# One iteration re-ordered in a convolution, attention and expert kernel: scores and weighted values pulled apart, the second residual moved to the next iteration, the first deviations sent through DRAM

## The chip, the cores and the metric

The kernel runs on one core of a Trainium2 chip (trn2). The core has a matrix engine (TensorE, PE in the profile, with its weight loads as PEld), a vector engine (VectorE, DVE), a scalar engine (ScalarE, ACT), GpSimd (POOL) and a sync engine (SyncE, SP) that here only starts DMAs; POOL starts some too. Each engine takes its own instructions strictly in their order and waits on semaphores for the others. [...] The metric is the time of one execution on the device in microseconds, the median over several runs.

## The reference, cut to what matters

The input x has the shape 32 x 56 x 56 x 128. Layer 0 is a group norm, a batch norm reduced to its sign, and a 3 x 3 convolution with binary inputs and binary weights, with a residual. Layer 1 takes the 3136 tokens of each image, does a window attention (64 tokens, 4 heads of 32, causal) with a residual, and then an expert layer in which each of 64 experts picks the 8 tokens of an image with the largest softmax over tokens.

```python
x = x + _L0_conv_ref(_gn(x), L0_conv_gamma, L0_conv_beta, L0_conv_W)
t = _to_tokens(x)
t = t + _L1_attn_ref(_ln_t(t), L1_attn_w_qkv, L1_attn_w_proj, L1_attn_b_proj)
t = t + _L1_ffn_ref(_ln_t(t), L1_ffn_gate_w, L1_ffn_gate_b, L1_ffn_weight1, L1_ffn_weight2)
...
def _ln_t(v, eps=1e-5):
    m = jnp.mean(v, axis=-1, keepdims=True)
    s = jnp.var(v, axis=-1, keepdims=True)
    return (v - m) / jnp.sqrt(s + eps)
```

The two layer norms matter here. The kernel has the mean folded into centred weights, so that of each norm only the reciprocal deviation of a token is left to be multiplied in.

## The kernel before

**Stages.** A first stage reads all of x once for the statistics of the norms (line 292 on). The main loop (line 933) then does convolution, attention, the second residual and the gate's logits. A last stage, from line 1029, does the experts and adds their outputs to the rows they were picked from. All of this document is about the main loop and its two ends.

**Blocks.** The images are taken in 16 pairs, and each pair in 7 blocks (NB) of 8 image rows, which is 448 tokens of each of two images. That gives 112 blocks. A block is held as 7 units (NU) of 128 columns, 64 tokens of the one image and 64 of the other. In most tiles channels are on the partitions, so a deviation, which belongs to a token, must be spread over 128 partitions before it can be multiplied in.

**The pipeline of blocks.** Iteration n works on several blocks at once: it loads block n+6, makes the binary inputs of n+5 (`bits`), convolves n+3 (`conv`, `residual`), takes the statistics of n+2 (`norm1`), multiplies the deviations into n+1 and makes its queries, keys and values (`normalise`, `queries_or_keys`, `values`), does the attention of block n (`scores`, `attend`, `turn_out`, `project`, `norm2`) and the gate's logits of n-1 (`gate_logits`). The order in which the methods are called is the order of the instructions on PE, DVE, ACT, POOL and SP, since in the fast form of the loop (line 373) nothing reorders them.

**What one block passes through.** `bits` transposes a loaded block on PE (xT_ps, line 440), ACT makes xT and the thresholded input bn, DVE turns that into bits (lines 496 and 497). `conv` does nine products into one PSUM bank (cv), four at one place of the iteration and five at another. `residual` takes the sums out of PSUM (ACT, s2; DVE, s1) and adds them to xT, which gives yT (line 526). `norm1` transposes yT on PE (yt), DVE takes the statistics (line 433 and four small ones), POOL raises the variance to the power -0.5 (line 426). `normalise` spreads the deviations by seven transposes of a broadcast column on PE (rr, line 537) and multiplies (n1T, line 541). `scores` adds a mask by four products and then the 56 products of queries and keys (sc); ACT takes exp (pT). `attend` multiplies with the values (av), DVE divides (rs, ao). `turn_out` transposes ao (aoT_ps, with a copy by ACT), `project` multiplies with the projection's weights (pj) and adds the second residual on DVE (tT, line 679). `norm2` transposes tT (tt), ACT copies it (tok), DVE and POOL take its deviations, and tok is stored twice by DMAs, to the output on POOL's queue and to a scratch copy (toks) on SP's. `gate_logits` multiplies tT with the gate's weights (lg, copied by ACT).

**Steps of a finished pair.** When a pair's last block is done, its logits are worked on beside the next pair's blocks, in steps numbered j = 1 to 13, one per iteration (`step`, line 898): j = 1 ends the spreading of the second deviations over DRAM (`spread`, drow), 2 scales 3136 logits per partition, 3 finds the 8 largest, 4 their positions, 5 gathers the rows by eight indirect DMAs on POOL, 6 takes their statistics and the exps, 7 weighs them, 8 to 13 build the matrix that spreads expert outputs to rows (`shares`). Steps 8 to 13 of a pair fall into the same iterations as steps 1 to 6 of the next.

**PSUM.** Two single banks are held by cv and by lg; lg's bank also serves two small transposes (dT_ps in `spread`, pl in `turn_pooled`). All other tiles of a block rotate through three places of two banks each (`bank2`), so a new tile waits until the third tile before it has been read. An iteration of before takes 12 such tiles, in the order sc, sc, rr, av, xT_ps, qT_ps, aoT_ps, kT_ps, v_ps, pj, yt, tt.

**Zeros.** The matrix share, in DRAM, must be zero before the shares are stored. In iterations 1 to 8 SP starts one DMA of 1 MB each for it (line 942).

Of the kernel before, what the change touches and what calls it, by code (L numbers as in the profile page):

```python
# [30 lines left out]
def kernel(  # L31
# [40 lines left out]

    ident = const.tile([P, P], F32, name="ident")
# [9 lines left out]
    head1 = const.tile([P, HEADS, HD], F32, name="head1")  # L83
# [12 lines left out]
    g4 = const.tile([P, P // 4, 4], F32, name="g4")  # L96
# [12 lines left out]
    tri = const.tile([P, 2, P], F32, name="tri")  # L109
# [54 lines left out]
    with tc.tile_pool(name="prep", bufs=1) as prep, tc.tile_pool(  # L164
# [123 lines left out]


        TP = 2 * S // P  # L290
        x2 = x.rearrange("b h w c -> (b h w) c").rearrange("(n p j) c -> n p j c", p=P, j=TP)
        for pr in range(NPAIR):
            xb = xs.tile([P, TP, C], F32, name="xb")
            nc.sync.dma_start(out=xb, in_=x2[pr])
            st = xs.tile([P, 2, NB, 6], F32, name="st")
            for g in range(NB):
                pt = xps.tile([P, 2, 512], F32, name="pt").rearrange("p a (s c) -> p (a s) c", c=P)
                for j in range(NU):
                    nc.tensor.transpose(pt[:, j, :], xb[:, g * NU + j, :], ident)
                for i in range(2):  # L300
                    nc.vector.bn_stats(st[:, i, g, :], pt[:, :NU, i * WIN : (i + 1) * WIN])  # L301
            for i in range(2):
                nc.vector.bn_aggr(
                    mv[:, 2 * pr + i, :], st[:, i].rearrange("p g s -> p (g s)")
                )
            if pr == NPAIR - 4:
                group_norm(0, B - 8)
            if pr == NPAIR - 2:
                scaled(0, B - 8)
        group_norm(B - 8, B)  # L310
# [20 lines left out]


# [3 lines left out]

    share = dram.tile([NQ, P, NPAIR, 2, ES], F32, name="share")
    toks = [dram.tile([2, S, P], F32, name=f"toks{i}") for i in range(NPAIR)]
    eout = dram.tile([E, B, P], F32, name="eout")
    obias_d = dram.tile([P, NG, P], F32, name="obias_d")  # L340
    devs = [dram.tile([2, NB * NU, WIN], F32, name=f"devs{i}") for i in range(NPAIR)]
# [25 lines left out]
    def main_loop(fast):  # L367
        with ExitStack() as main:
# [41 lines left out]
            zero = first.tile([P, 4 * P], F32, name="zero")  # L410
            nc.gpsimd.memset(zero, 0.0)
# [46 lines left out]
            class Block:  # L458
# [16 lines left out]
                def bits(self):  # L475

                    pr, r = self.pr, self.r
                    xT_ps = turn(self.xb, "xT_ps")
                    self.xT = xTp.tile([P, 2, BT], F32, name="xT")
                    nc.scalar.activation(  # L480
                        self.xT.rearrange("c i (p j) -> c i p j", j=NU),
                        units(xT_ps).rearrange("c j (i p) -> c i p j", p=WIN),
                        AF.Identity, bias=conv_nb,
                    )
                    bn = w1.tile([P, 2, RB, W], F32, name="bn")
                    for i in range(2):
                        b = 2 * pr + i
                        nc.scalar.activation(  # L488
                            bn[:, i].rearrange("c h (g j) -> c h g j", j=NU),
                            units(xT_ps)[:, :, i * WIN : (i + 1) * WIN].rearrange(  # L490
                                "c j (h g) -> c h g j", h=RB
                            ),
                            AF.Identity, bias=thr_b[:, b : b + 1], scale=thr_a[:, b : b + 1],
                        )
                    bit = w1.tile([P, RB, W], FP16, name="bit")
                    nc.vector.tensor_scalar(bit, bn[:, 0], 0.0, 1.0 / FINE, ALU.is_ge, ALU.mult)
                    nc.vector.scalar_tensor_tensor(
                        hbits[pr % 2][:, 1 + r * RB : 1 + (r + 1) * RB, 1 : 1 + W],
                        bn[:, 1], 0.0, bit, ALU.is_ge, ALU.subtract,
                    )  # L500
# [15 lines left out]
                def residual(self):  # L516

                    cv = self.cv[:, :BT]
                    self.yT = yTp.tile([P, NU, P], F32, name="yT")

                    s2 = w1.tile([P, BT], I32, name="s2")
                    nc.scalar.activation(s2, cv, AF.Identity, bias=conv_mid)  # L522
                    s1 = w1.tile([P, BT], F32, name="s1")
                    nc.vector.tensor_sub(s1, s2, cv)  # L524
                    for i, t in enumerate((s1, s2)):
                        nc.vector.scalar_tensor_tensor(  # L526
                            of_image(self.yT, i), windows(t), conv_s2[:, i : i + 1],
                            windows(self.xT[:, i, :]), ALU.mult, ALU.add,
                        )

                def norm1(self):
                    self.rstd1 = unit_stats(units(turn(self.yT, "yt")), "ln1")

                def normalise(self):
                    rr = bank2("rr")
                    for u in range(NU):
                        nc.tensor.transpose(  # L537
                            units(rr)[:, u, :], self.rstd1[:, u : u + 1].to_broadcast([P, P]), ident
                        )
                    self.n1T = w1.tile([P, NU, P], F32, name="n1T")  # L540
                    nc.vector.tensor_mul(self.n1T, units(rr), self.yT)
# [125 lines left out]
                def project(self):  # L667

                    pj = bank2("pj")
                    for g in range(2):  # L670
                        for i in range(2):
# [4 lines left out]
                            )  # L676
                    self.tT = w1.tile([P, NU, P], F32, name="tT")
                    for i in range(2):
                        nc.vector.scalar_tensor_tensor(  # L679
                            of_image(self.tT, i), windows(pj[:, i, :BT]), bproj_c,  # L680
                            of_image(self.yT, i), ALU.add, ALU.add,
                        )
# [24 lines left out]
            class Pair:  # L707
# [9 lines left out]
                def spread(self, r0, r1):  # L717
# [4 lines left out]
                    dT = wp.tile([m, P], F32, name=f"dT{m}")  # L722
# [7 lines left out]
                    for i in range(2):  # L730
                        nc.sync.dma_start(
                            out=self.drow[i * E : (i + 1) * E, r0 * BT : r1 * BT],
                            in_=devs[self.pr][i : i + 1, r0 * NU : r1 * NU]
                            .rearrange("o m t -> o (m t)").to_broadcast([E, (r1 - r0) * BT]),
                        )
# [131 lines left out]
                def shares(self, ks):  # L867

                    if ks[0] == 0:
                        self.sh = gatep.tile([P, E, K], F32, name="sh")  # L870
# [27 lines left out]
                def step(self, j):  # L898
# [13 lines left out]
                    elif j == 8:  # L912
                        self.pool()
                        if self.pr < NPAIR - 2:
                            self.shares(range(0, 2))
                    elif j == 9:
                        self.shares(range(2, 3))
                    elif j == 10:
                        self.shares(range(3, 4))
                    elif j == 12:  # L920
                        self.shares(range(4, 6))
                    elif j == 13:
                        self.shares(range(6, 8))
# [9 lines left out]
            for n in range(-6, N + 1):  # L933
                this, nxt, conv, prev = at(n), at(n + 1), at(n + 3), at(n - 1)
# [4 lines left out]
                if at(n + 6):  # L939
                    at(n + 6).load()  # L940
                if 0 < n <= NQ:
                    nc.sync.dma_start(
                        out=share[n - 1].rearrange("p n i s -> p (n i s)").rearrange(
                            "p (a s) -> p a s", s=4 * P
                        ),
                        in_=zero.unsqueeze(1).to_broadcast([P, NPAIR * 2 * ES // (4 * P), 4 * P]),
                    )
# [20 lines left out]
                if n == N - 4:  # L968
                    parts = [Part(0, early)]
                    parts[0].load1()  # L970
                    parts[0].load2()
                if this:
# [3 lines left out]
                if nxt:  # L976
                    nxt.normalise()
                if prev:
                    prev.gate_logits(pairs[prev.pr])
                if 5 in ends:  # L980
                    ends[5].gather()
                if 7 in ends:
                    ends[7].put_rows()
                if this:
                    this.attend()
                if at(n + 5):
                    at(n + 5).bits()
# [6 lines left out]
                if 1 in ends and n < N:  # L994
                    ends[1].spread(NB - 1, NB)
                if nxt:
                    nxt.queries_or_keys(0)
                if this:
                    this.turn_out()
                if nxt:  # L1000
                    nxt.queries_or_keys(1)
                    nxt.values()
                if 8 in ends:
                    ends[8].turn_pooled(pcv.tile([P, 512], F32, name="pl", tag="lg")[:, :P])
                if 6 in ends:
                    ends[6].exps()
                for j, pair in steps:
                    pair.step(j)
                if n == N - 1:
                    pairs[this.pr].scale(0, NB - 2)  # L1010
                    pairs[this.pr].largest(0, NB - 2)
                if this:
                    this.project()
                if at(n + 2):
                    at(n + 2).norm1()
                if conv:
                    conv.conv(4, NTAP)
                    conv.residual()
                if this:
                    if this.r == 0:  # L1020
                        pairs[this.pr] = Pair(this.pr)
                    this.norm2(pairs[this.pr])
# [212 lines left out]
```

## Time and profile before

| | |
|---|---|
| median of 5 runs | 2471.09 us (2462.24 to 2475.05) |
| the profiled execution | 2466.99 us, of which the span is 2465.3 us |
| PE busy | 2177.6 us, 88% of the span |
| DVE busy | 1781.1 us, 72% |
| ACT busy | 1158.0 us, 47% |
| POOL busy | 814.4 us, 33% |
| granted clock of PE, mean | 0.95 |
| first stage | up to about 165 us |
| main loop, from the first weighted values (av) of block 0 to the last | 203 to 2168 us |

The page of the profile divides the span into 40 slices of 61.6 us; in the main loop PE is at 9 tenths or more in each of them. In the timeline a row is a run of equal instructions: its start, its length, the engine, the line, and in brackets the engine's idle time before it and who ended it. Matmuls overlap at their ends, so what a group costs PE is the distance from its start to the start of the next row.

### The profile page before, as it was taken

What the parts mean: (1) busy time and instruction counts of PE and PEld (TensorE: products, weight loads), DVE (VectorE), ACT (ScalarE), POOL (GpSimd) and SP (SyncE); (2) the same over time, 40 slices, a digit from 0 to 9 for tenths busy, and PEclk for the clock granted to TensorE, in tenths of its full rate; (3) what the DMA queues carried; (4) which work ended last, traced back from release to release, by engine and by line L of the source; (5) the groups of instructions that cost most, each with busy time, mean ns of one, the idle gap of its engine ahead of it and who ended that gap; (6) DMA issues with size and microseconds to landing.
All of it is one profiled execution on the core that took longest, in us unless ns stands there. A gap on an engine that the chain in (4) does not pass through costs nothing.

```text
span 2465.3 us, 82834 instructions
## 1 busy us (share of the span) xinstructions
PE 2177.6 (88%) x35865; PEld 1529.7 (62%) x35865; DVE 1781.1 (72%) x4974; ACT 1158.0 (47%) x1683; POOL 814.4 (33%) x772
## 2 busy tenths in 40 slices
PE   6769999999999999999999999999999999936342
PEld 5656666667676766676766666666666666613232
DVE  8965667777788878787877787878787878773221
ACT  0015555555555555555555555555555555422110
POOL 1011224232333333333332323233323232333555
PEclk9989999999999999999999999999999999967766
DMA  9933454645354545454544444545444444648762
GB/s 375 386 130 93 136 154 99 129 95 117 92 115 100 114 97 115 97 117 98 116 99 111 101 106 103 114 103 115 101 109 101 111 104 97 209 122 292 252 217 81
DMA packets 238300, 334.31 MB, mean 136 GB/s; under 512 B 50598, under 2 KB 175206, under 8 KB 231654
## 3 DMA queue, kind: packets, MB, share of 16 engines
q1 hardware_dynamic: 208102, 255.48, 37.1%
q0 software_dynamic: 27648, 72.38, 12.5%
q8 instruction: 285, 4.67, 0.8%
q10 hardware_dynamic: 2176, 1.05, 0.1%
q14 instruction: 89, 0.73, 0.1%
HBM read 195.14 MB, written 134.74 MB: 134 GB/s over the span
## 4 chain that ended last, share of the span: by engine, by line
PE 74%; DVE 7%; issue 6%; ACT 6%; POOL 5%; DMA 1%; POOLq 0%; SPq 0%; DVEq 0%; another core or an unknown queue 0%
PE cv L509 8%; PE av L639 8%; PE kT_ps L550 8%; PE pj L673 8%; PE v_ps L566 7%; PE sc L590 6%; POOL out_dram L1129 4%; PE xT_ps L440 4%; PE lg L701 4%; PE yt L440 4%; PE rr L537 4%; PE tt L440 4%; ACT bn L488 3%; DVE st L301 3%; PE qT_ps L550 3%
## 5 line engine op out<-in xcount | busy, mean ns | idle before, releaser
L426 POOL TENSOR_TENSOR ln_rstd<-ln_var,nhalf 128x7 f32<-128x7 f32 x112 | 167.6, 1496 | 960.1 <-DVE ln_var L423 615.4
L480 ACT ACTIVATE xT<-xT_ps,conv_nb 128x896 f32<-128x896 f32 x112 | 112.8, 1007 | 407.2 <-PE xT_ps L440 251.3
L426 POOL TENSOR_TENSOR devs<-ln_var,nhalf 128x7 f32<-128x7 f32 x112 | 165.7, 1479 | 268.9 <-DVE ln_var L423 268.9
L605 ACT ACTIVATE pT<-sc 128x896 f32<-128x896 f32 x224 | 193.3, 915 | 120.2 <-PE sc L590 120.2
L639 PEld LDWEIGHTS av<-vblk,pT 64*64 64x64 f32 x12544 | 195.5, 135 | 86.0 <-ACT pT L605 73.0
L509 PE MATMUL cv<-hbits,wconv 128*128 128x448 f16 x1008 | 236.8, 362 | 12.7 <-DVE s L524 6.3
L566 PEld LDWEIGHTS v_ps<-wqkvT,n1T 128*128 128x128 f32 x1568 | 192.7, 192 | 41.6 <-issue 41.6
L639 PE MATMUL av<-vblk,pT 64*64 64x33 f32 x12544 | 209.4, 221 | 6.0 <-issue 5.1
L522 ACT ACTIVATE s<-cv,conv_mid 128x448 int32<-128x448 f32 x112 | 70.8, 632 | 297.5 <-PE cv L509 219.6
L679 DVE SCALAR_TENSOR_TENSOR tT<-pj,bproj_c,yT 128x448 f32<-128x448 f32 x224 | 142.7, 679 | 92.5 <-PE pj L673 78.6
L550 PE MATMUL kT_ps<-n1T,wqkvT 128*128 128x448 f32 x448 | 197.7, 564 | 5.8 <-issue 1.3
L673 PE MATMUL pj<-aoT,wprojT 64*128 64x448 f32 x896 | 198.7, 562 | 1.1 <-ACT aoT L665 1.1
L566 PE MATMUL v_ps<-wqkvT,n1T 128*128 128x128 f32 x1568 | 193.1, 275 | 0.0
L550 PE MATMUL qT_ps<-n1T,wqkvT 128*128 128x448 f32 x448 | 188.3, 543 | 0.0
L433 DVE BATCH_NORM_STATS2 ln_st<-yt 128x6 f32<-128x128 f32 x784 | 165.5, 283 | 29.0 <-PE tt L440 14.6
L590 PE MATMUL sc<-qT,kT 32*64 32x64 f32 x12544 | 170.3, 238 | 0.5 <-issue 0.5
L692 POOL DMA_DIRECT2D out_dram<-tok x224 | 169.1, 756 | 0.1
L590 PEld LDWEIGHTS sc<-qT,kT 32*64 32x64 f32 x12544 | 154.4, 133 | 23.7 <-issue 23.7
L433 DVE BATCH_NORM_STATS2 ln_st<-tok 128x6 f32<-128x128 f32 x784 | 161.9, 278 | 4.9 <-ACT tok L687 4.9
L1129 POOL DMA_INDIRECT out_dram<-f_rows,rowidx x128 | 123.8, 967 | 103.3 <-DVE f_rows L1125 66.7
L488 ACT ACTIVATE bn<-xT_ps,thr_b,thr_a 128x448 f32<-128x448 f32 x224 | 149.3, 720 | 2.7 <-DVE thr_b L330 2.6
L526 DVE SCALAR_TENSOR_TENSOR yT<-s,conv_s,xT 128x448 f32<-128x448 f32 x224 | 143.5, 682 | 4.0
(187 smaller groups left out, 4094.4 us busy)
## 6 DMA issues: line engine op xcount, KB each, us to landing
xb<-in_x_dram SPq DMA_DIRECT2D x16, 3136.0 KB
xb<-in_x_dram SPq DMA_DIRECT2D x224, 224.0 KB
toks<-tok SPq DMA_DIRECT2D x224, 224.0 KB
out_dram<-tok POOLq DMA_DIRECT2D x224, 224.0 KB
u<-in_L_ffn_weight_dram SPq DMA_DIRECT2D x16, 2048.0 KB
drow<-devs SPq DMA_DIRECT2D x30, 672.0 KB
share<-zero SPq DMA_DIRECT2D x8, 1024.0 KB
grows<-rows SPq DMA_DIRECT2D x32, 256.0 KB
```

What stands on the lines that cost most here:

```text
L426: nc.gpsimd.tensor_tensor(rstd, var, nhalf[:, :n], ALU.pow)
L433: nc.vector.bn_stats(st[:, u, :], src[:, u, :])
L440: nc.tensor.transpose(units(t)[:, u, :], src[:, u, :], ident)
L488: nc.scalar.activation(bn[:, i].rearrange("c h (g j) -> c h g j", j=NU), units(xT_ps)[:, :, i * WIN : (i + 1) * WIN].rearrange("c j (h g) ...
L509: nc.tensor.matmul(self.cv[:, :BT], lhsT=wconv[:, t, :], rhs=hb[:, r * RB + kh : r * RB + kh + RB, kw : kw + W], start=(t == 0), stop=(t = ...
L550: nc.tensor.matmul(pp[:, a, :BT], lhsT=wqkvT[:, s, :], rhs=flat[:, a * BT : (a + 1) * BT], start=True, stop=True,)
L566: nc.tensor.matmul(units(vp)[:, u, :], lhsT=self.n1T[:, u, :], rhs=wqkvT[:, 2, :], start=True, stop=True,)
L590: nc.tensor.matmul(tiles[h // 2][part, h % 2, u * WIN : (u + 1) * WIN], lhsT=left[hp, u, part], rhs=right[hp, u, part], start=False, stop= ...
L605: nc.scalar.activation(pT, rows2(sc), AF.Exp, scale=HD ** -0.5)
L639: nc.tensor.matmul(av[h % 2 * WIN : (h % 2 + 1) * WIN, i, m * VW : (m + 1) * VW], lhsT=self.pT[h // 2][rows, h % 2, u, :], rhs=self.vb[row ...
L673: nc.tensor.matmul(pj[:, i, :BT], lhsT=wprojT[rows, g, :], rhs=self.aoT[rows, :, g, :], start=(g == 0), stop=(g == 1),)
L1129: put = nc.gpsimd.indirect_dma_start(out=of, out_offset=bass.IndirectOffsetOnAxis(ap=rowidx[:, n, q : q + 1], axis=0), in_=rows[q][:, n, : ...
```

## The change

The order of the calls within an iteration is new, and with it the distance of the blocks: the load is at n+7, bits at n+6, the convolution at n+4; the residual, the statistics of the first norm and their deviations are at n+3.

- **Scores and weighted values.** Between the scores of block n and its weighted values (av) now stand half of the convolution, the transposes of tT of block n-1 (tt) and of a loaded block (xT_ps), and the queries and keys of block n+1. The values of block n+1 come after.
- **Second residual.** `project` only makes the product pj. The residual itself is a new method `finish`, called at the start of the next iteration, followed there by `norm2` and `gate_logits` of that block.
- **Convolution's residual.** It is cut in two: `sums` reads PSUM in the convolution's own iteration, `residual` adds in the next.
- **First deviations.** `norm1` now takes the columns of yT with a step of seven tokens, so that the 128 x 7 deviations lie in token order, and POOL's queue stores them to DRAM (rdev). One iteration later `spread1`, on the same queue, loads them to all 128 partitions (rr, now in SBUF, 3584 bytes per partition). `normalise` multiplies yT by it. The seven transposes of line 537 are gone, and an iteration has 11 tiles in the rotation.
- **Steps of a pair.** Steps 1 to 7 (scale, largest, positions, statistics, weigh) stand between queries and keys and the weighted values, and so ahead of DVE's rs and ao; steps 8 to 13 (`step2`) stand ahead of s1. The shares are divided differently over them. The exps stand ahead of the exps of the scores on ACT.
- **The rest.** The zeros of share are written by eight DMAs at the end of the first stage. The loads of `drow` are cut into pieces of at most two blocks. Several tiles have moved between pools.

```diff
+        for q in range(NQ):
+            nc.sync.dma_start(out=share[q].rearrange("p n i s -> p (n i s)"), in_=zero)
         group_norm(B - 8, B)
...
                 def norm1(self):
-                    self.rstd1 = unit_stats(units(turn(self.yT, "yt")), "ln1")
+
+                    yt = bank2("yt")
+                    flat = self.yT.rearrange("c u p -> c (u p)").rearrange("c (p u) -> c u p", u=NU)
+                    for u in range(NU):
+                        nc.tensor.transpose(units(yt)[:, u, :], flat[:, u, :], ident)
+                    nc.gpsimd.dma_start(out=rdev[self.n], in_=unit_stats(units(yt), "ln1"))
+
+                def spread1(self):
+
+                    self.rr = w2.tile([P, NU, P], F32, name="rr")
+                    nc.gpsimd.dma_start(
+                        out=self.rr.rearrange("c u p -> c (u p)"),
+                        in_=rdev[self.n].rearrange("(o p) u -> o (p u)", o=1).to_broadcast([P, P * NU]),
+                    )
 
                 def normalise(self):
-                    rr = bank2("rr")
-                    for u in range(NU):
-                        nc.tensor.transpose(
-                            units(rr)[:, u, :], self.rstd1[:, u : u + 1].to_broadcast([P, P]), ident
-                        )
                     self.n1T = w1.tile([P, NU, P], F32, name="n1T")
-                    nc.vector.tensor_mul(self.n1T, units(rr), self.yT)
+                    nc.vector.tensor_mul(self.n1T, self.yT, self.rr)
...
+                def finish(self):
+
                     self.tT = w1.tile([P, NU, P], F32, name="tT")
...
+                if prev:
+                    if prev.r == 0:
+                        pairs[prev.pr] = Pair(prev.pr)
+                    prev.finish()
                 if this:
                     this.scores()
                 if conv:
                     conv.conv(0, 4)
                 if nxt:
                     nxt.normalise()
+                if at(n + 3):
+                    at(n + 3).residual()
                 if prev:
-                    prev.gate_logits(pairs[prev.pr])
+                    prev.norm2(pairs[prev.pr])
+                if at(n + 2):
+                    at(n + 2).spread1()
                 if 5 in ends:
                     ends[5].gather()
...
+                if at(n + 6):
+                    at(n + 6).bits()
+                for s in range(2):
+                    if nxt:
+                        nxt.queries_or_keys(s)
+                for j, pair in steps:
+                    pair.step(j)
                 if this:
                     this.attend()
-                if at(n + 5):
-                    at(n + 5).bits()
+                if prev:
+                    prev.gate_logits(pairs[prev.pr])
                 if this and this.r == NB - 1 and n < N - 1:
                     pairs[this.pr].spread(0, NB - 1)
...
                 if 1 in ends and n < N:
                     ends[1].spread(NB - 1, NB)
+                if at(n + 3):
+                    at(n + 3).norm1()
+                if 8 in ends:
+                    ends[8].turn_pooled(pcv.tile([P, 512], F32, name="pl", tag="lg")[:, :P])
                 if nxt:
-                    nxt.queries_or_keys(0)
+                    nxt.values()
                 if this:
                     this.turn_out()
...
+                if conv:
+                    conv.conv(4, NTAP)
+                    conv.sums()
+                if 6 in ends:
+                    ends[6].exps()
                 if this:
                     this.project()
```

## The prediction

> **What bounds the kernel now.** I read the shares of the page, then the main loop as one stretch, then PE's timeline of one iteration, and after that the rows of what the change moves. The line of the main loop has its length, then busy times of PE, weight loads, DVE, ACT and POOL, PE's granted clock, the share of the DMA engines and GB/s.
>
> ```profile
> PE 2177.6 (88%) x35865; PEld 1529.7 (62%) x35865; DVE 1781.1 (72%) x4974; ACT 1158.0 (47%) x1683; POOL 814.4 (33%) x772
> ```
> ```profile
> 203.00:2062.00 1859.00, 1818.77 (x32173) 1265.61 (x32172) 1445.66 (x4174) 1033.64 (x1330) 613.38 (x569) 0.99 0.47 110
> ```
> ```profile
> 482.42 0.59 PE L579 MATMUL sc<-masks,selw 64*128 64x448 bf16 x4
> ...
> 485.11 0.93 PE L537 MATMUL rr<-ident,ln_rstd 128*128 128x128 f32 x7
> 485.96 0.97 PE L701 MATMUL lg<-tT,gateT 128*64 128x448 f32 x4
> 486.87 1.84 PE L639 MATMUL av<-vblk,pT 64*64 64x33 f32 x112
> 488.63 0.98 PE L440 MATMUL xT_ps<-ident,xb 128*128 128x128 f32 x7
> 489.45 1.67 PE L550 MATMUL qT_ps<-n1T,wqkvT 128*128 128x448 f32 x4
> 490.96 0.93 PE L662 MATMUL aoT_ps<-ident,ao 128*128 128x128 f32 x7
> 491.94 1.77 PE L550 MATMUL kT_ps<-n1T,wqkvT 128*128 128x448 f32 x4
> 493.55 1.72 PE L566 MATMUL v_ps<-wqkvT,n1T 128*128 128x128 f32 x14
> 495.21 1.77 PE L673 MATMUL pj<-aoT,wprojT 64*128 64x448 f32 x8
> 496.91 0.98 PE L440 MATMUL yt<-ident,yT 128*128 128x128 f32 x7
> 497.73 1.12 PE L509 MATMUL cv<-hbits,wconv 128*128 128x448 f16 x5
> 498.69 0.93 PE L440 MATMUL tt<-ident,tT 128*128 128x128 f32 x7
> ```
>
> The reader is to see that PE has no gap: each group starts where the last ends, and attention starts at 486.87, 504.01 and 521.12, 17.13 us apart. 105 iterations from 203.0 take 1859 us, 17.71 each. The missing 0.57 per iteration, 4.0 per pair of images, is nearly all in one iteration of seven, j = 5, with the gather on POOL: it lasts 18.8 to 22.5 us. There PE, DVE and ACT wait while the gather is issued, and what delays them the trace does not say:
>
> ```profile
> 405.72 0.36 PE L579 MATMUL sc<-masks,selw 64*128 64x448 bf16 x2
> 407.80 0.36 PE L579 MATMUL sc<-masks,selw 64*128 64x448 bf16 x2 [1.72 <-DVE ln_st L433]
> ```
>
> So PE is the bound, and DVE, with 1446 of 1859 us (13.8 per iteration), is the next.
>
> **The change part by part.** I lay the new order out with the start-to-start times of that timeline, t = 0 at the masks: masks 0, scores 0.52, cv 1.91, tt 2.69, xT_ps 3.55, queries 4.37, keys 5.88, av 7.49, lg 9.25, yt 10.16, values 10.98, aoT_ps 12.64, cv 13.50, pj 14.46, end 16.16.
>
> *Transposes of rr gone.* 485.96 - 485.11 = 0.85 us x 112 = 95 us, all on PE's path. aoT_ps to kT_ps took 0.98 where other groups of seven transposes take 0.82 to 0.86, since keys waited for bn's PSUM place; keys now need tok's, read by 4.6. Another 0.12 x 112 = 13.
>
> *aoT close to pj.* ACT starts a copy 0.16 us after its matmuls' successor starts (v_ps: 495.21, copy 495.37), and takes 0.91. The copy of aoT runs 13.66 to 14.57, pj could start at 14.46: 0.16 x 112 = 18 us lost. Before, two groups lay between.
>
> *lg close to the small transposes.* `spread` now follows `gate_logits` directly and shares its single bank. lg ends 10.31, ACT's copy of 0.53 (line 705) ends 10.84, so PE stands 0.73 us, twice per pair: 1.5.
>
> *DVE's order.* After pj: tT 1.3, n1T, yT, then the statistics of tok (copied by 4.6) to 6.7, bits to 7.4, a step of the pair, then rs and ao (1.5 us, not before av ends at 9.4). aoT_ps needs ao at 12.64, so a step may last 3.7 us. Scale and largest (3.42) fit, and so do the row statistics of j = 6 (8 x 0.21 + 0.7). The positions do not:
>
> ```profile
> 509.68 3.42 DVE L770 FIND_INDEX8 idx<-top,logits 128x8 uint32<-128x3136 f32 x1
> ```
>
> With their small ones they ran from 509.61 to 514.17, 4.56 us: ao is ready at 13.5, 0.9 late. Weighing (j = 7, 4.1 us) is 0.5 late, but falls into the iteration whose `spread` has already stopped PE. Steps 8 to 13 have until 17.6 before tT holds up tt; three shares (3 x 1.31 after 13.2, then s1) exceed that by 0.2. With the lg waits 2.6 per pair, x 15 = 39 us. Bounds: 0 if the waits fall together, and 1.5 us in each of the five iterations that hold a long step, 112 us. I take 39, since its terms come from rows of the same operations. n1T reads two SBUF tiles; scale (3419 ns for 3136) gives 0.98, the row of n1T is 1.08. DVE has room, so nothing.
>
> *The trip over DRAM.* POOL gets two DMA issues more per iteration: by line 692 0.76 us each; it was busy 5.8 of 17.7 us. The store stands behind `norm1`'s power (14.8) and has until the next iteration's t = 10. The load is issued behind norm2's power and two stores of tok, at about 10, and n1T wants it at 17.6. From the rows
>
> ```profile
> 488.53 1.48 POOL L692 DMA_DIRECT2D out_dram<-tok  x2
> ```
> ```profile
> 491.00:492.00 1.00, 0.94 (x9) 0.70 (x7) 0.47 (x2) 1.00 (x3) 0.00 (x0) 1.00 0.72 186
> 492.00:493.00 1.00, 1.00 (x3) 0.62 (x4) 1.00 (x2) 1.00 (x2) 0.00 (x0) 1.00 0.19 64
> ```
>
> the stores' last bytes move 2.3 us after the second issue ends. Behind them come 128 rows of 3584 bytes; at the rate of drow's packets in this trace (10,752 bytes in 0.77 us) eight per DMA engine take 2.1 us. With the load's own issue and an estimated 0.5 for its completion it has landed by about 15. Nothing is queued behind a late load but n1T, and behind that DVE's whole order. Likely cost zero; bounds 0, and 1 us in every iteration (112) if it lands 4 us later than this. Its 51 MB over the loop, 13% of the DMA engines' time by that rate, meet a share of 0.47.
>
> *Strided loads of yT.* The weights of yt are now read with a step of 28 bytes. The nearest row is hT_ps, which loads hs with a step of 16 bytes, beside contiguous f_sh, both in the last stage at the lower clock:
>
> ```profile
> L1076 PEld LDWEIGHTS hT_ps<-ident,hs x64: 195/226/231, 2222.4 to 2409.3; 128*128 128x128 f32 x64
> L1120 PEld LDWEIGHTS fo<-logits,f_sh x256: 186/256/338, 2240.5 to 2440.6; 128*128 128x128 f32 x128
> ```
>
> Minimum, median and maximum in ns: no dearer. I take zero; the upper bound is a load doubled by 0.14 us, 7 x 0.14 x 112 = 110 us. [...]
>
> *Gather.* Its eight issues (1.25 us apart) now run from 10.7 to t = 4.5 of the next iteration, past more hand-overs that PE waits for (ao, aoT, tT). The present price is 3.1 us per pair; unexplained, it may go (-3.1) or double (+3.1). I take +1, so 15 us. Power and store of `norm1` behind it end by 7, before the load at 10. j = 6 reads the rows at 7.4, when they have just landed. The exps (2.9) now delay pT to 4.1, and queries need it at 4.37: covered, by 0.3.
>
> *Both ends.* Block 0's deviations were ready at 189.5 and n1T began at 191.06; two issues and two landings of 2.3 make that 195.6. One block more is convolved by then (some 1 us returned): +4. The zeros, 8.4 MB at the 0.084 us that a packet of 2048 bytes took, are 21.5 us of DMA from 143 (where the loads of x end) to 165, with the first blocks landing near 168; the thresholds they wait for are ready at 170.8. Zero, and up to 20 if writing runs at half that rate. On SP the stores of toks move with norm2 to mid-iteration and drow takes eight issues per pair for four (about 0.62 us each, line 692's row there); the next block's load stands behind them and is needed 19 us after its issue, so nothing waits. The last stage keeps its order: 0, within 3.
>
> Sum: -95 - 13 + 18 + 39 + 4 + 15 = -32. The profiled execution took 2467.0, so 2435; the median stands 4.1 above it: **2439 us**.
>
> **The rivals.** *A: the DRAM trip becomes the loop.* n1T, yT, the statistics, the power, the two stores and the next load follow each other: 1.1 + 1.2 + 2.9 + 1.5 + 1.5 + 0.75 + landing 4.2 = 13.2 of 16.2 us. From a landing of 7.2 on, each further microsecond costs 112 us; at 8.5 the time is 2439 + 146, about 2585, at 7.7 about 2495, slower. For it: POOL's strict order. Against: the 2.3 us above.
>
> *B: DVE becomes the bound.* 13.3 us plus its exposed waits; if five iterations in seven lose 1.5 us, that is 112 instead of DVE's 17 in the sum, and it ends near 2534, with half of it near 2478. For it: slacks of 0.2 to 1.7 us. Against: its busy sum stays below 16.2.
>
> *C: the strided loads cost.* 2439 + 110 = 2549.
>
> *D: the paybacks are hidden.* Only aoT and the ends stay: 2471 - 108 + 22 = 2385.
>
> **How the numbers follow.** Main case 0.48 (2410 to 2465), A 0.13, B 0.19, C 0.07, D 0.13. The range leaves out half of D below and C with the worse half of A above: 2388 to 2515. Half a per cent, 12 us, is about what a measurement can tell from no change. Faster: D, the main case but for its top, and a little of B: 0.60. Same: 0.14, from B and the main case. Slower: 0.26.
>
> **What would show it.** Right: no line 537, yt's groups still 0.82 apart, attention about 16.3 us apart in quiet iterations, PE waiting 0.15 for ACT's aoT and 0.7 for lg's copy, DVE's n1T not waiting for a DMA. Wrong: n1T waiting on a load each iteration (A), aoT_ps waiting on ao in most iterations (B), yt's loads near 280 ns (C), or a gather iteration above 24 us.

## The result, and the profile after

The changed kernel took 2467.71 us (median of 36 runs, 2456.98 to 2475.01), the kernel before 2466.61 us beside it (62 runs): a ratio of 1.000, 95% interval 0.999 to 1.0009. The forecast was 2439 us, faster. What was to be saved was saved, and something took it back.

The page's shares after, and the main loop as one stretch (same columns as before):

```profile
PE 2100.2 (85%) x35081; PEld 1468.5 (60%) x35081; DVE 1774.7 (72%) x4974; ACT 1146.9 (47%) x1683; POOL 988.4 (40%) x996
```
```profile
203.00:2062.00 1859.00, 1744.84 (x31564) 1208.56 (x31564) 1442.17 (x4180) 1024.60 (x1332) 774.53 (x781) 0.98 0.51 131
```

PE is busy 77 us less over the whole run, as the missing products of rr foretold, but the span is the same 2465 us: PE now stands idle for that time. One quiet iteration of PE's timeline after:

```profile
719.86 0.55 PE L599 MATMUL sc<-masks,selw 64*128 64x448 bf16 x4
...
722.52 0.93 PE L448 MATMUL tt<-ident,tT 128*128 128x128 f32 x7
723.29 0.93 PE L448 MATMUL xT_ps<-ident,xb 128*128 128x128 f32 x7
724.05 1.67 PE L570 MATMUL qT_ps<-n1T,wqkvT 128*128 128x448 f32 x4
...
729.82 1.13 PE L548 MATMUL yt<-ident,yT 128*128 128x128 f32 x7
730.79 1.73 PE L586 MATMUL v_ps<-wqkvT,n1T 128*128 128x128 f32 x14
732.43 0.95 PE L682 MATMUL aoT_ps<-ident,ao 128*128 128x128 f32 x7
733.22 1.12 PE L517 MATMUL cv<-hbits,wconv 128*128 128x448 f16 x5
734.44 1.77 PE L692 MATMUL pj<-aoT,wprojT 64*128 64x448 f32 x8
736.04 0.54 PE L599 MATMUL sc<-masks,selw 64*128 64x448 bf16 x4
```

From masks to masks 16.18 us, against 17.13 before. So the quiet iteration is a little better than forecast (16.32). The loss is in particular iterations, those with a step of a finished pair. Taking the start of attention (av) in every block, and the median over the pairs for each place in the pair:

| iteration | before | after | forecast for after |
|---|---|---|---|
| quiet | 17.13 | 16.15 to 16.2 | 16.3 |
| the two with `spread` | 17.16, 17.40 | 16.96, 17.02 | 0.73 each over quiet |
| positions (j = 4) | 17.14 | 17.39 | 0.9 over quiet |
| gather (j = 5) | 19.97 | 22.79 | 1 more over quiet than before |
| sum of a pair | 123.1 | 122.7 | 121 |

In the gather's iteration the excess over a quiet one rose from 2.8 to 6.6 us. PE's waits after (engine, line, releaser; total, times, longest) and its timeline in one gather show where:

```profile
PE sc L610 <- issue: 41.4, 77, 1.1
...
PE dT_ps L743 <- ACT logits L727: 22.5, 31, 0.7
PE aoT_ps L682 <- DVE ao L671: 21.5, 19, 3.1
PE pj L692 <- ACT aoT L685: 12.5, 15, 1.1
```
```profile
786.93 0.93 PE L610 MATMUL sc<-qT,kT 32*64 32x64 f32 x32
788.96 0.30 PE L610 MATMUL sc<-qT,kT 32*64 32x64 f32 x3 [1.10 <-issue]
789.69 0.21 PE L610 MATMUL sc<-qT,kT 32*64 32x64 f32 x1 [0.43 <-issue]
790.41 0.46 PE L610 MATMUL sc<-qT,kT 32*64 32x64 f32 x3 [0.51 <-issue]
791.12 0.26 PE L610 MATMUL sc<-qT,kT 32*64 32x64 f32 x1 [0.25 <-issue]
791.84 1.52 PE L610 MATMUL sc<-qT,kT 32*64 32x64 f32 x72 [0.45 <-issue]
```

The scores, 112 short matmuls that take 1.5 us elsewhere, now fall into the gather, whose issues run from 780.3 to 790.8. From 788.96 on they advance in steps of 0.72 us, by one to three matmuls a step, and only 1 us behind the last issue does PE run freely again. No engine is named as the releaser. In the old order the scores came just behind the gather: in the profile before, one gather's issues run from 396.3 to 406.1, and the scores begin at 408.1.

### The profile page after: what moved, and what is told of

Its sections match the earlier page's. It is cut to its first block, busy times and chain, and to the rows that moved or that the text cites. A ratio compares the mean times of both kernels' runs of the same rounds, so it can differ in the third digit from the quotient of the medians.

```text
span 2465.2 us, 81828 instructions
## 1 busy us (share of the span) xinstructions
PE 2100.2 (85%) x35081; PEld 1468.5 (60%) x35081; DVE 1774.7 (72%) x4974; ACT 1146.9 (47%) x1683; POOL 988.4 (40%) x996
## 3 DMA queue, kind: packets, MB, share of 16 engines
q8 instruction: 279, 4.57, 0.8%
## 4 chain that ended last, share of the span: by engine, by line
PE 63%; DVE 12%; issue 9%; ACT 8%; POOL 4%; DMA 2%; another core or an unknown queue 1%; SPq 1%; ACTq 0%; POOLq 0%; DVEq 0%
PE pj L692 8%; PE sc L610 8%; PE av L659 6%; PE v_ps L586 6%; PE qT_ps L570 6%; PE kT_ps L570 6%; PE cv L517 4%; ACT aoT L685 4%; PE yt L548 4%; POOL out_dram L1159 4%; PE lg L723 3%; PE xT_ps L448 3%; DVE st L308 3%; PE tt L448 3%; ACT vblk L590 2%
## 5 line engine op out<-in xcount | busy, mean ns | idle before, releaser
L434 POOL TENSOR_TENSOR devs<-ln_var,nhalf 128x7 f32<-128x7 f32 x112 | 178.5, 1594 | 698.2 <-DVE ln_var L431 689.1
L434 POOL TENSOR_TENSOR ln_rstd<-ln_var,nhalf 128x7 f32<-128x7 f32 x112 | 174.4, 1557 | 402.3 <-DVE ln_var L431 402.0
L517 PE MATMUL cv<-hbits,wconv 128*128 128x448 f16 x1008 | 243.5, 370 | 14.2 <-DVE s L531 8.6
L610 PE MATMUL sc<-qT,kT 32*64 32x64 f32 x12544 | 198.1, 239 | 43.1 <-issue 41.4
L610 PEld LDWEIGHTS sc<-qT,kT 32*64 32x64 f32 x12544 | 169.0, 135 | 97.4 <-issue 97.4
L590 ACT COPY vblk<-v_ps 128x896 f32<-128x896 f32 x112 | 101.5, 907 | 244.5 <-PE v_ps L586 238.0
L570 PE MATMUL kT_ps<-n1T,wqkvT 128*128 128x448 f32 x448 | 186.6, 539 | 0.0
L586 PEld LDWEIGHTS v_ps<-wqkvT,n1T 128*128 128x128 f32 x1568 | 186.1, 193 | 0.8 <-issue 0.7
L826 POOL DMA_INDIRECT rows<-toks,pairidx x128 | 138.5, 1082 | 45.7 <-issue 38.4
L727 ACT COPY logits<-lg 128x448 f32<-128x448 f32 x112 | 59.7, 533 | 203.7 <-PE lg L723 203.7
```

Of the source, the lines that this page charges most:

```text
L434: nc.gpsimd.tensor_tensor(rstd, var, nhalf[:, :n], ALU.pow)
L517: nc.tensor.matmul(self.cv[:, :BT], lhsT=wconv[:, t, :], rhs=hb[:, r * RB + kh : r * RB + kh + RB, kw : kw + W], start=(t == 0), stop=(t = ...
L570: nc.tensor.matmul(pp[:, a, :BT], lhsT=wqkvT[:, s, :], rhs=flat[:, a * BT : (a + 1) * BT], start=True, stop=True,)
L586: nc.tensor.matmul(units(vp)[:, u, :], lhsT=self.n1T[:, u, :], rhs=wqkvT[:, 2, :], start=True, stop=True,)
L590: nc.scalar.copy(self.vb[:, :, :, :HD], units(vp).rearrange("p u (h d) -> p u h d", d=HD))
L610: nc.tensor.matmul(tiles[h // 2][part, h % 2, u * WIN : (u + 1) * WIN], lhsT=left[hp, u, part], rhs=right[hp, u, part], start=False, stop= ...
```

## The experiments

**Theory G**: the gather took the gain: 3.8 us per pair more than before, 57 us in fifteen pairs. **Rivals**: the stall belongs to the iteration (DVE's shares, PE's new order) and not to the gather; each of the eight issues has its price wherever it stands; or the gain was lost somewhere else.

**The gather replaced by one load**, after and before.

```
-  for k in range(K):
-      nc.gpsimd.indirect_dma_start(out=self.rows[:, k, :], ...)
+  nc.gpsimd.dma_start(out=self.rows, in_=toks[pr][0, 0:1, :].unsqueeze(1).to_broadcast([P, K, P]))
```

> The changed kernel with the gather's eight indirect DMAs replaced by one plain POOL DMA that reads one fixed token's row into all of rows (so the pooled rows and what follows from them are not the reference's; the same bytes land). Theory G (the gather is where the gain went): the iteration of j = 5, now 22.8 us from attention to attention, falls to the 16.2 of a quiet one, 6.6 x 15 = 99 us, so about 2369. Rival S (the stall is the iteration's own, from DVE's shares or PE's new order, and the gather only stands beside it): j = 5 stays above 20 us, and the time within 15 us of 2468.

> The kernel before with the same replacement (pooled rows not the reference's). Theory G: j = 5, 20.0 us, falls to 17.15, 2.85 x 15 = 43 us, so about 2424; with a_one_load the pair shows what the change is worth without a gather, 2369 - 2424 = -55 us. Rival S: no change, 2467; then the change is worth 0 with or without a gather.

Measured: 2424.4 and 2476.12 us, beside a kernel before of 2379.39 (ratios 1.0207, 1.0173 to 1.0242, and 1.0411, 1.0388 to 1.0434). Neither theory: the replacement costs more than what it replaces, so it can't tell G from S. The profile says why. The load, 512 KB that are one row of 512 bytes read 1024 times, needs 16.4 us to land (rr's 448 KB need 5.0 in the same run), and at the end of thirteen of the first fifteen PE stops once, for 1.8 to 9.7 us, with no releaser. PE's timeline in a_one_load, 10 us after a load began at 527.5:

```profile
536.71 0.60 PE L448 MATMUL xT_ps<-ident,xb 128*128 128x128 f32 x4
544.84 0.90 PE L448 MATMUL xT_ps<-ident,xb 128*128 128x128 f32 x3 [7.52 <-issue]
```

The trace's DMA records have two queues of the kind instruction, and the larger one, q8, moved 4.57 MB in 279 fetches (16.4 KB each). It has 16 us between two fetches here (526.0 and 542.2), against a median of 6.8 us in the main loop, and PE goes on 2.6 us after the second. Of the other fourteen stops of over 1.6 us in the main loop, thirteen end 2.2 to 2.5 us after a fetch that came 12 to 21 us behind the last; b_one_load's trace has the same sign. From these times I take q8 to bring PE's instructions, and this load to starve PE of them. The gather's stall looks different: several small steps, and PE moves on at each with no fetch between them (in the stall of 788 to 791.8 in the result's profile the last fetch had come at 783.75), so late instructions are not its cause. And the runs told something else: the kernel before took 2379 us here, not 2467.

**The gather split, and the gather earlier.** Set against the same runs of the kernel before.

```
-  if 5 in ends: ends[5].gather()
+  if 5 in ends: ends[5].gather(0, K // 2)       # a_split; row statistics at j = 7
+  if 6 in ends: ends[6].gather(K // 2, K)
```
```
   if at(n + 3): at(n + 3).norm1()
+  if 4 in ends: ends[4].gather()                # a_gather_behind_store, instead of j = 5
```

> The changed kernel with four of the eight indirect DMAs at j = 5 and four at j = 6 (row statistics move to j = 7, weighing behind the projection's transposes). In the trace after, PE runs 6 to 8 us into the gather without a stop and is then cut to some 5 records per 0.74 us in the scores until the gather ends. Theory L (only work with many short instructions, running late in the gather, is cut): four issues end at about t = 15.9, before the scores at 16.7, so j = 5 and j = 6 each stay below 18 us and the time falls by 60 to 95 us, to 2373 to 2408. Rival E (each issue has its own price, wherever it stands): the 6.6 us only spread over two iterations, 2468 within 15.

> The changed kernel with all eight issues some 5 us earlier, at j = 4 behind norm1's store: they start about 1 us before the scores and run to about t = 9.6 of the next iteration, through tt, xT, queries, keys and the whole of av (7.5 to 9.3). Theory L as built-up delay (the first 5 us of a gather do no harm): the scores run in 1.5 us, av is cut late in the gather by 1 to 3 us, 2385 to 2440. Theory D (any dense work beside a gather is cut from its first issue): scores at 5 records per 0.74 us would last to the end of the gather, so the iteration grows by 7 us or more over a quiet one, 2470 or more.

Measured: 2340.67 us (ratio to before 0.9843, 0.9821 to 0.9866) and 2335.75 us (0.9817, 0.9796 to 0.9838). Both lie below everything that any of the theories allowed (2373 at the least for the one, 2385 for the other), and the base had moved as well by 88 us. So they say nothing of L, E or D: a changed kernel on the same chip was missing.

**Both kernels again, with profiles.** The two kernels as they are, on one chip.

> The changed kernel once more, beside the same runs of the kernel before as the three that follow (the runs of the first four experiments had a kernel before of 2379 us, 88 below the 2467 of the result, so a common base is needed). If the gather costs the same on whatever chip: as long as the kernel before within 0.5%, with 22.8 us in the iteration of j = 5. If its price is the chip's: j = 5 nearer to 18, and the changed kernel 1 to 3% faster than the one before.

> The kernel before with a profile on the same chip, to see which part of it differs from its first profile: the last stage (clock 0.68 there), or the iterations of the gather (20.0 us). If the gather costs the same on whatever chip, 20.0 stays and any difference lies in the last stage.

Measured: after 2329.26 us, before 2376.76 us beside it, ratio 0.9802 (0.9779 to 0.9825); the profiled kernel before 2379.36. Here the change is worth 2%, about what was forecast and more. The gather's iteration takes 16.5 us after and 17.2 before: hardly more than a quiet one. The stretch of one gather, engine by engine (length, then busy PE, weight loads, DVE, ACT, POOL; PE's clock, DMA share, GB/s). First the changed kernel in the result's profile, then on this chip:

```profile
780.27:791.80 11.53, 7.84 (x82) 4.92 (x80) 9.65 (x24) 2.35 (x3) 9.37 (x9) 0.93 0.37 112
```
```profile
759.43:771.00 11.57, 11.44 (x177) 8.28 (x176) 10.79 (x30) 6.05 (x8) 9.41 (x9) 1.00 0.37 109
```

The kernel before, in its first profile and on this chip:

```profile
396.28:407.80 11.52, 9.74 (x58) 6.14 (x57) 3.87 (x13) 5.08 (x8) 7.71 (x8) 1.00 0.31 78
```
```profile
396.10:407.60 11.50, 11.44 (x173) 7.82 (x172) 5.68 (x19) 6.77 (x10) 8.97 (x9) 1.00 0.30 77
```

POOL issues its eight DMAs in the same 10 to 11 us in all four, and the DMA engines move as many bytes at the same share. Only the others differ: in the result's profiles PE, ACT and DVE get less done in the same stretch. A second sign is in the records of semaphore updates. The result's profile of the changed kernel has 5.4 per us in its gathers (before: 6.0), and this one 17.7 (before: 16.3). But one program makes the same updates wherever it runs, and for the kernel before the whole trace has 25,591 records in the first profile and 29,188 here. The missing ones stand beside indirect DMAs: 1130 against 2981 in the fifteen gathers and 2 us behind each, 1448 against 3306 from the last stage's first indirect store on, and the rest is equal within 0.5%. So the low rate shows records that were lost, not updates that were rare. On this chip the scores beside the gather lose 0.4 us in all:

```profile
764.88 0.55 PE L599 MATMUL sc<-masks,selw 64*128 64x448 bf16 x4
765.35 1.89 PE L610 MATMUL sc<-qT,kT 32*64 32x64 f32 x112
767.17 0.94 PE L517 MATMUL cv<-hbits,wconv 128*128 128x448 f16 x4
```

The 90 us between the two profiles of before fall into two halves. From first to last attention it is 1962.3 against 1915.8 us, 47 us, of which 15 gathers of 2.8 us are 42. From there to the end it is 300 against 256, where POOL issues the indirect stores of the results. PE's granted clock over that stretch was nearly the same, 0.68 against 0.70. What differs is again how an engine gets on beside indirect DMAs. DVE's two steps behind the same products, while POOL issues sixteen stores, first in the first profile of before and then on this chip:

```profile
2255.11 1.24 DVE L1102 TENSOR_TENSOR os<-op,drow 32x128 f32<-32x128 f32 x4 [5.63 <-remote]
2265.11 0.69 DVE L1069 COPY hs<-hp 128x512 f32<-128x512 f32 x1 [8.76 <-remote]
```
```profile
2203.59 1.24 DVE L1102 TENSOR_TENSOR os<-op,drow 32x128 f32<-32x128 f32 x4 [0.54 <-PE op L1096]
2204.87 1.29 DVE L1069 COPY hs<-hp 128x512 f32<-128x512 f32 x2
```

"Remote" means that the trace has no update on record which ended the wait; PE's products were done 5.2 us before the first of these steps, and DVE got to the second 1.3 us after the last store was issued. Such waits add up to 95 us in the first profile's last stage, and here there are none. For the changed kernel the difference from first to last attention is 1954.2 against 1862.4, 92 us, and 15 gathers that cost 6.6 - 0.35 us more are 94. Theory G holds: where the gather doesn't stall the engines, the same program has the gain. This compares two sets of runs; no run moved the gather or the scores under the conditions of the result.

**One part undone.** norm1's deviations over seven transposes on PE again, no trip over DRAM.

```
-  nc.gpsimd.dma_start(out=rdev[self.n], in_=unit_stats(units(yt), "ln1"))
+  self.rstd1 = unit_stats(units(yt), "ln1")
...
+  rr = bank2("rr")
+  for u in range(NU):
+      nc.tensor.transpose(units(rr)[:, u, :], self.rstd1[:, u : u + 1].to_broadcast([P, P]), ident)
```

> The changed kernel with norm1's deviations spread by seven transposes on PE again and no trip over DRAM (one part undone). By the prediction's term: 0.85 x 112 = 95 us more than the changed kernel on the same chip (up to 108 if keys wait for a PSUM place again). Rival P (the gain of that part is lost behind something else): under 40 us more. Rival Q (POOL's two issues per iteration delay what PE waits for, and the gather starts earlier without them): no slower than the changed kernel.

Measured: 2430.45 us, 101 us over the changed kernel on the same chip, and 1.0233 (1.0216 to 1.025) of the kernel before. P and Q fall. The trip over DRAM is worth 101 us, and the rest of the change costs 54: more than half of the gain is paid back, on a chip without the stall too.

**The paybacks taken away.** First all of them (a_all: split gather; spread, positions and weighing moved). Then, with the changed kernel beside them on the next chip, spread and the small steps of the positions (a_late), the same with the gather at j = 4 (a_late_behind), and the split again.

```
-  (spread's calls ahead of norm1)
   if this: this.turn_out()
+  (spread's calls)
...
   elif j == 4:
-      self.tokens()            # search and small steps, ahead of attend
+      self.find()              # the search; the small steps go to step2
```

> The changed kernel with the gather split over j = 5 and 6, spread moved behind the projection's transposes, and the positions (j = 4) and weighing (j = 7) behind the same transposes. If the four waits named in the trace after are each what they seem: 6.4 (gather) + 1.6 (spread, twice 0.8) + 1.2 (positions) per pair, 9.2 x 15 = 138 us under the changed kernel on the same chip. If moving them only hands them on: less than half of it, under 69 us.

> The changed kernel as the common base of this set. If this chip is like that of the result (the kernel before at about 2467): equal to the kernel before, with 22.8 us in the iteration of j = 5 and updates of semaphores at some 5 per us in the gather. If it is like the two others (the kernel before at about 2377): 2% faster, 16.5 us there and some 17 updates per us. A mixture would speak against one cause for both.

> The changed kernel with spread moved behind the projection's transposes and, of the positions, only the search (3.4 us) left ahead of attend, its small steps (1.1 us) behind the same transposes. If spread's wait for lg's copy and the wait of ao are what they seem: 1.6 + 1.2 per pair, x 15 = 42 us under the changed kernel of this set. If the moved steps are only paid elsewhere (s1 and tT behind the small steps, drow later): under 15 us.

> a_late with all eight indirect DMAs at j = 4 behind norm1's store, some 5 us earlier. Where the gather costs 6.6 us per pair at j = 5 (kernel before at 2467), this takes 6.0 of them away as long as only dense work late in a gather is cut: 90 us under a_late. Where it costs 0.35 (kernel before at 2377), it is worth nothing or loses up to 1 us per pair, as a_gather_behind_store's 117.3 us per pair against the changed kernel's 116.5 showed: 0 to 15 us over a_late.

> The split gather once more, now with the changed kernel beside it. Where the gather costs 6.6 us per pair: 60 to 95 us under the changed kernel, unless each issue has its own price (then the same). Where it costs 0.35: no gain, and the row statistics and weighing, which now share an iteration (17.4 us and more against 16.2), make it 10 to 25 us slower.

Measured: a_all 2324.89 us, 4 under the changed kernel (2329.26) of its chip, within the scatter of the runs. Of the 138 us expected 96 were the gather's, which on this chip had hardly a price; of the other 42 it kept 4 (the split itself costs 11 in the next set). On the next chip the changed kernel takes 2328.35 (0.9781, 0.9765 to 0.9797), a_late 2316.52 (0.9738, 0.9721 to 0.9755), a_late_behind 2315.31 (0.9733, 0.9713 to 0.9752), the split 2338.95 (0.9827, 0.981 to 0.9843). So a_late gains 12 us, as the rival had it, of the 42 that the waits seem to be worth. The places show what became of each. The positions' iteration falls from 17.39 to 16.25, and the second spread's from 17.03 to 16.43, as expected. The first spread's stays (17.0 and 17.2), because there the weighing of j = 7 keeps ao, and so aoT_ps, late; the prediction had said of that wait that it was covered by spread's stop, and with the stop gone it is the bound. That makes 26 us by the places, of which single long iterations took back a part. The split costs 11 us where the gather costs next to nothing: row statistics and weighing share an iteration of 17.4 us and more, and in a_split DVE's scale (line 775) once stands 21.4 us for drow.

**The strided loads.** norm1's transposes read yT in order.

```
-  nc.tensor.transpose(units(yt)[:, u, :], flat[:, u, :], ident)
+  nc.tensor.transpose(units(yt)[:, u, :], self.yT[:, u, :], ident)
```

> The changed kernel as the common base of this set. As in after_third: 2% under the kernel before where its gather iteration takes 16.5 us, level with it where that takes 22.8; which of the two it is, the kernel before (2377 or 2467) says as well.

> The changed kernel with norm1's transposes reading yT in order instead of with a step of 28 bytes (the deviations then reach the wrong tokens, so everything behind norm1 is not the reference's; no instruction is added or left out). If the step is what makes yt's group last 0.96 us against 0.77 of aoT_ps and its loads 216 ns against 141: the group falls to about 0.80 and the kernel by 0.16 x 112 = 18 us under the changed kernel of this set. If the step costs nothing, as the prediction had it, and 0.96 is due to the group's place: no change within 5 us.

> The kernel with spread and the positions' small steps late and the gather at j = 4, beside the changed kernel. Where the gather costs 6.6 us per pair at j = 5 (kernel before at 2467): 42 + 90 = 130 us under the changed kernel if only dense work late in a gather is cut, 42 if each issue has its own price wherever it stands. Where it costs 0.35: 13 us under, as in the set before (2315 against 2328).

Measured: after 2325.78 us (0.9772, 0.9739 to 0.9804), contiguous 2322.48 (0.9764, 0.9734 to 0.9794), a_late_behind 2318.79 (0.9747, 0.972 to 0.9775), 7 us under after. The weight loads, minimum, median and maximum in ns, in after_fourth and then in a_contiguous:

```profile
L548 PEld LDWEIGHTS yt<-ident,yT x784: 197/216/232, 182.2 to 2030.6; 128*128 128x128 f32 x196
```
```profile
L547 PEld LDWEIGHTS yt<-ident,yT x784: 137/140/231, 182.2 to 2028.9; 128*128 128x128 f32 x196
```

The step costs 76 ns per load, and yt's group takes 0.96 us against 0.82. But only iterations in which DVE has no long step get shorter (16.13 to 15.98, and the gather's 16.51 to 16.38). With scale, search or weighing on DVE, ao comes no sooner, and aoT_ps waits away what yt saved (16.20 and 17.38 as before). 3 us of 18: the two medians' intervals overlap.

## Why the prediction was wrong, and where it was right

*The step that failed: gather.* "The present price is 3.1 us per pair; unexplained, it may go (-3.1) or double (+3.1). I take +1, so 15 us." In the runs of the result it rose by 3.8 per pair, 57 us, past the upper bound of 46.5; that is 42 us more than taken. The bound scaled an unexplained wait by itself. It should have come from the work that was newly put beside the gather: the scores, which I had laid out at t = 16.7, inside its 10.7 to 20.7. The prediction's own sign, "a gather iteration above 24 us", was set too high; 22.8 was already more than twice the old excess over a quiet 16.2. On the three later chips that ran both kernels the term is 0.35 per pair, 5 us, and the change measures 0.977 to 0.980 where 2439 of 2471 is 0.987.

*Sum of the result.* Against the forecast's -32: gather +42, the quiet iterations about -19 (0.97 each instead of the 0.80 that -95 - 13 + 18 makes), the ends +4 (av of block 0 starts 8.8 us later, and 0.8 is won behind the last), and one stop of 10.1 us that begins near 466 us, where before has one of 3.3: +7. That makes +2, good to a few us; measured 0. The stop is one for late instructions, as in a_one_load: it ends 2.2 us after a fetch that came 22 us behind the last (before: 2.4 us, 13 us), beside SP's DMAs into obias_d. The prediction has no term for it.

*rr and keys, -108*: right. 101 us when undone alone, and PE is busy 77 us less. aoT_ps fell from 0.98 to 0.79, 0.19 for 0.12; tt, xT_ps and pj are 0.06 to 0.10 shorter each, which was not forecast.

*aoT close to pj, +18*: right in kind. Five taps of cv before pj now take 1.22 us from start to start, 0.96 before: 0.26 for 0.16.

*lg and DVE's order, +39*: right. 0.8 and 0.85 us for the two spreads, less the 0.26 that before had lost there, and 1.2 for the positions instead of 0.9: 2.6 per pair, as forecast. Whether three shares cost their 0.2 can't be told. *D* falls with this: the paybacks are there.

*Trip over DRAM, 0*: right; A falls. n1T waits for rr 16 or 17 times in a whole run, by 0.2 to 2.9 us, nearly always in the iteration behind a gather, which holds POOL's store up. The 0.5 us for the load's completion was an estimate that no row of before shows; in the result's profile n1T starts 0.3 to 1.0 us behind the load's last packet in those waits (median 0.6). *B* falls too: DVE is no busier, and its late ao shows only with the long steps.

*Strided loads, 0*: too low. I took hT_ps for the nearest row, but its loads (226 ns) stood beside a contiguous row that was no faster (256), in a stage with a lower clock (0.68, against 0.99 in the main loop), and so gave no sign of the difference. With the step of 28 bytes a load pays 76 ns on top of 140, not the doubling of the upper bound, and of the 18 us that this could cost the run without the step won 3, so *C* falls as well.

*What stays open.* Why the other engines were slowed beside indirect DMAs in the runs of the result, and not on four chips later, is not settled. Nothing in the DMA's or POOL's own times differs. The record doesn't name the chip of the result, so it isn't shown that the chip makes the difference, nor whether the stall and the lost records have one cause. No later set met the stall. So theories L, E and D were never put to the test, and neither was whether the gather at j = 4 (a_late_behind) takes the 6.6 us back, though it costs nothing against a_late and lets the scores begin 0.7 us ahead of the gather. The fastest version run is a_late_behind, with a_late beside it within 1 us: 0.973 and 0.975 of the kernel before on two chips, and 13 and 7 us under the changed kernel.

## What to carry to other kernels

When work is moved, look first at what now runs beside the stretch whose stalls are unexplained, and bound the new stall by that work, not by the old stall. A gain that is certain on one engine (101 us here) may be half spent by the order that makes room for it; undo the parts singly to see both. And take both kernels along in every set of runs: a base from another set would have shown a gain of over 5% here that was 2%. Before a count of records is read as a rate, compare its total between two profiles of one program.

## What the runs showed of the hardware

- While POOL issued eight indirect DMAs (10 to 11 us), PE did 7.84 us of work in 11.53 in one profile (after) and 11.44 in 11.57 in another of the same program (after_again), with POOL's time (9.37 and 9.41) and the DMA share (0.37) equal. In the first, PE advanced through short matmuls in steps of 0.72 us.
- In the same set (before), DVE stood 5.63 and 8.76 us beside sixteen indirect stores, where it waited 0.54 us and not at all in a later set (before_again); PE's granted clock was 0.68 and 0.70. Records of semaphore updates were missing there: 25,591 of them against 29,188.
- Beside a load of 512 KB that read one row of 512 bytes in DRAM 1024 times (16.4 us to land), the fetches of q8 came 16 us apart at one stop, where the main loop's median is 6.8, and PE stopped up to 9.7 us, to go on 2.2 to 2.6 us after a fetch (a_one_load).
- Weight loads of 128 x 128 in fp32 with a step of 28 bytes took 216 ns (after_fourth), contiguous ones 140 (a_contiguous; medians).
